# Scan inputs by VectorE for 20 of 32 units of a sequence, with scan tiles in place in a ring

## The chip, the cores and the metric

The program runs on one core of a Trainium2 chip (trn2). The metric is the device time of one execution in microseconds, as the median of several executions. One execution is also taken with a hardware profiler, which gives the page and the trace quoted here. The engines go by short names: PE is TensorE's matmuls and PEld its weight loads, DVE is VectorE, ACT is ScalarE, POOL is GpSimd and SP is SyncE, which here only issues DMAs.

## What is computed

The reference runs four blocks on four sequences of 256 tokens with width 512: latent attention, a gated feed-forward layer, a selective state-space layer, and a mixture of low-rank experts. The change is in the state-space layer, whose core is

```python
proj = hidden_states @ in_proj_w                 # x and z, 1024 channels each
xc = silu(causal_conv(x, taps=4) + conv_b)
ssm_p = einsum('bdl,ed->ble', xc, x_proj_w)      # 32 + 16 + 16 rows
dt_r, Bm, Cm = (rmsnorm(part) for part in split(ssm_p))
dt = softplus(einsum('blr,dr->bdl', dt_r, dt_proj_w) + dt_bias)
def step(h, inp):                                # h: 1024 channels x 16 states
    h = exp(dt_t[..., None] * A) * h + dt_t[..., None] * B_t[:, None, :] * x_t[..., None]
    return h, einsum('bdn,bn->bd', h, C_t)
y = (ys + D * xc) * silu(z)
```

Everything is in float32.

## The kernel before, in words

Attention and the feed-forward layer take the first third of the time; their last down-projection (L469) runs on into the first scans. After that the program is one loop over 128 *units* (`for u in range(total)`, L1342), 32 for each of the four sequences. A sequence has 8 chunks `c` of 128 channels; a chunk has 4 units `k` of 32 channels. A unit holds 32 channels x 4 state groups on the 128 partitions and 4 states x 256 time steps along the free dimension, so each of its tiles is 128 x 1024.

A unit goes through five steps:

- `decays(u)` on ScalarE (L967): four exponentials of dt times A, out of `dts`, which `spread` (L934) brings from DRAM as dt copied to the four state groups. They are emitted two units ahead.
- `scan_in(u)` on TensorE (L977): the input dt * x * B. `step_x` (L912, GpSimd) makes du = dt * x for a chunk, `step_turn` (L920) turns it with TensorE into `dut`, and 32 small matmuls of `dut` with `bdg`, a tile of B on diagonals that `b_diag` (L874) makes for each sequence, write the tile `bx` in PSUM. It has two buffers and is emitted one unit ahead.
- `scan(u)` on VectorE (L995): the recurrence over time, from `decay` (SBUF) and `bx` (PSUM) into `h` (SBUF).
- The product with C on GpSimd (L1000): `hc` = `h` * `crows`, where `c_rows` (L884, L887) spreads the rows of C over the partitions.
- `states_sum(q)` on TensorE (L1009), once for four units: sums over states into `ysum` (one PSUM tile), then `take_sum` on VectorE (L1014) adds D * xc. It is emitted in iteration 4q+5.

Around these, the loop has lists of other work for the next sequence and the previous one: `px_mm` (L759) and `pz_mm` (L942), the input projections; the convolution, `conv_in`, `conv_taps` and `conv_out`, whose mode is chosen by chunk (four matmuls with diagonals on TensorE at L815; three products on ScalarE at L803 and three sums on GpSimd at L818; or three multiply-adds on VectorE at L820); `pp_mm` (L845) with its norm; `step` (L900, L904), the step sizes with a softplus; `router`, `dense` and `expert_out` for the experts (L1030, L1096, L1101); `gate` (L1019); and the output projection `out_mm` (L1112). The order is written out by hand: `put(b, s, f, ...)` sets in which iteration, relative to sequence `b`, a piece is emitted. `first_at` pieces come first, then `decays(u+2)`, `scan_in(u+1)`, `soon_at` and `at` pieces, `scan(u)`, the sum, then `late_at` pieces. Each engine runs its pieces in that order. SP's queue is in order too: spreads of dt, weight loads of 512 KB (`w_in`), sends of dt to DRAM and results all stand in one row.

Of the kernel before, what the change touches and what calls it, by code (L numbers as in the profile page):

```python
# [28 lines left out]
NG = 4  # L29
# [12 lines left out]
def block_kernel(  # L42
# [587 lines left out]
    lnw = we.tile([64, 1], F32, name="lnw")  # L630
    dtw = we.tile([RK, DIN], F32, name="dtw")
# [15 lines left out]
    psx = ctx.enter_context(tc.tile_pool(name="psx", bufs=2, space=PSUM))  # L647
# [12 lines left out]
    def load_rest():  # L660
# [7 lines left out]
        nc.sync.dma_start(lnw, lnw_d)  # L668
        nc.sync.dma_start(dtw, dtw_d)
# [5 lines left out]
    csel = w1.tile([64, NU, P], F32, name="csel")  # L675
    nc.vector.tensor_copy(
        csel.rearrange("p g (n j) -> p (g n) j", n=NG),
        ident[0:64, RK + NST : RK + 2 * NST].unsqueeze(2).to_broadcast([64, NST, NB]),
    )
# [22 lines left out]
    ysum = psy.tile([P, S], F32, name="ysum")  # L702

    def odd(b):

        return act if b % 2 else w1

# [20 lines left out]
    def norm_scale(b):  # L728
# [4 lines left out]
        for i in range(2):  # L733
            t = act.tile([P, D], F32, tag="xnt", name="xnt", bufs=2)
# [28 lines left out]
    def mode(b, p, i):  # L763

        if b == 0:
            return "dve" if i == 0 else "act"
        return "pe" if i == 0 else "act" if p < 2 else "dve"
# [18 lines left out]
    def conv_in(b, p):  # L786
# [7 lines left out]
        for i in range(2):  # L794
# [5 lines left out]
            if m == "act":  # L800
                tp = live["tap"] = four()[:, 0 : (KC - 1) * S].rearrange("p (k t) -> p k t", k=KC - 1)
# [4 lines left out]
    def conv_taps(b, p):  # L806
        pad = pads[p % 2]
        for i in range(2):
            c, m = 2 * p + i, mode(b, p, i)
            xc = xcs[b][:, c, :]  # L810
            for k in range(KC if m == "pe" else KC - 1):
# [5 lines left out]
                elif m == "act":  # L817
                    nc.gpsimd.tensor_tensor(xc, xc, live["tap"][:, k, :], ALU.add)  # L818
# [22 lines left out]
    def pp_mm(b, h):  # L841
        if h == 0:
            live["pp"] = psmm.tile([P, 2, S], F32, tag="mm", name="pp")
        for c in range(h * HALF, (h + 1) * HALF):
            mm(live["pp"][:64, 0, :], lhsT=xpw[:, c, :], rhs=xcs[b][:, c, :],  # L845
               start=(c == 0), stop=(c == DC - 1))

    def pp_square(b):
        pp = live["pp"]
        sq = w1.tile([P, S], F32, tag="sq", name="sq")[:64]  # L850
        nc.scalar.activation(sq, pp[:64, 0, :], AF.Square)
        mm(pp[:64, 1, :], lhsT=cst[:64, C_BLK : C_BLK + 64], rhs=sq, start=True, stop=True)
        live["rs"] = w1.tile([P, S], F32, tag="sq", name="rs1")[:64]
        inv_root(live["rs"], pp[:64, 1, :], eps[:64, 1:2])

    def pp_norm(b):
        rs = live["rs"]
        nrms[b] = w1.tile([64, S], F32, tag="nrm", name="nrm")
        nc.vector.scalar_tensor_tensor(
            nrms[b], live["pp"][:64, 0, :], lnw[:, 0:1], rs, ALU.mult, ALU.mult  # L860
        )

    def b_turn(b):

        bt = live["bt"] = psmm.tile([P, 4, 8], F32, tag="mm", name="pbt")
        for t in range(4):
            for r in range(2):
                mm(bt[r * HT : (r + 1) * HT, t, :], lhsT=nrms[b][:, t * HT : (t + 1) * HT],
# [12 lines left out]
    def c_rows(b, i):  # L881
# [595 lines left out]
```

## Time and profile before

| What | Value |
|---|---|
| Median of 3 runs | 912.42 us (912.37 to 913.72) |
| Profiled execution, its own time | 917.66 us |
| Span in the profile | 915.9 us |
| Mean granted TensorE clock | 0.972 |
| Scans run from / to (starts) | 332.5 / 904.4 us |
| Scan (L995), one unit | 2.28 us, 128 units |
| Product with C (L1000), one unit | 2.37 us |
| Scan input (L977), all units | 149.1 us of TensorE |
| VectorE's wait for ysum ahead of L1014 | 146.8 us, 32 times |

The page gives busy time by engine, then slices of the span, then groups of instructions: line, engine, operation, tiles out<-in, shapes, count, then busy us and mean ns of one, then idle time just before them and what ended it. The stage view gives, for each stretch of the span, the busy time of each engine in it with the count of instructions, the granted clock, and the share and rate of DMA. The source view gives min/median/max ns of a line's instructions. The timeline gives start, duration, and how many neighbours are merged (x2).

### The profile page before, as it was taken

How to read it: one execution, taken by the hardware profiler on the slowest of the kernel's cores; microseconds unless marked ns; L12 is line 12 of the kernel's file. 1: busy time of each engine (PE TensorE's matmuls, PEld its weight loads, DVE VectorE, ACT ScalarE, POOL GpSimd, SP SyncE). 2: the span in 40 equal slices, each digit the busy share in tenths (PEclk: the TensorE clock that was granted, in tenths of full speed). 3: DMA queues.
4: the chain of work that ended last, by engine and by line, in shares of the span. 5: the costliest groups of instructions: out<-in, count | busy, mean ns of one | idle time of the engine just before them, and what ended most of it. 6: DMA issues, size and time to landing. Idle time of an engine off the chain costs nothing.

```text
span 915.9 us, 27817 instructions
## 1 busy us (share of the span) xinstructions
PE 860.5 (94%) x12468; PEld 556.3 (61%) x12468; DVE 530.8 (58%) x530; ACT 498.8 (54%) x985; POOL 443.9 (48%) x349
## 2 busy tenths in 40 slices
PE   5999999999999999999799999989999989898996
PEld 2665546665557677777555777545677645565553
DVE  4587554687344435657647647635565645656664
ACT  4335574345563753656773765764565665347541
POOL 3233320013332223685657676654576636657775
PEclk8899999999999989999999999989999989999899
DMA  6233420012333222344341350132323104021200
GB/s 207 80 108 94 119 73 12 1 35 70 81 85 107 38 74 79 96 131 126 103 136 43 95 152 26 48 105 61 102 81 97 29 23 128 26 82 49 59 4 25
DMA packets 48482, 70.74 MB, mean 77 GB/s; under 512 B 10173, under 2 KB 30409, under 8 KB 48234
## 3 DMA queue, kind: packets, MB, share of 16 engines
q1 hardware_dynamic: 38570, 48.77, 18.5%
q0 software_dynamic: 9072, 18.35, 7.1%
q8 instruction: 98, 1.61, 0.7%
q10 hardware_dynamic: 720, 1.84, 0.6%
q14 instruction: 22, 0.18, 0.1%
HBM read 52.42 MB, written 7.34 MB: 65 GB/s over the span
## 4 chain that ended last, share of the span: by engine, by line
PE 40%; ACT 4%; DVE 4%; POOL 3%; issue 1%; POOLq 0%; ACTq 0%; DVEq 0%
PE bx L977 9%; PE ysum L1009 6%; PE po L1112 5%; PE pz L942 5%; PE px L759 3%; PE po L1096 3%; DVE h L995 3%; PE ptu L920 3%; POOL hc L1000 2%; ACT decay L967 2%; PE pc L815 1%; PE pp L845 1%; DVE bdg L874 1%; PE pcr L884 1%; PE pdt L900 1%
## 5 line engine op out<-in xcount | busy, mean ns | idle before, releaser
L1000 POOL TENSOR_TENSOR hc<-h,cr 128x1024 f32<-128x1024 f32 (+1 forms) x130 | 302.3, 2333 | 221.3 <-PE ysum L1009 138.8
L995 DVE TENSOR_TENSOR_SCAN h<-decay,bx 128x1024 f32<-128x1024 f32 (+1 forms) x129 | 284.1, 2226 | 51.9 <-PE bx L977 36.6
L967 ACT ACTIVATE decay<-dts,aneg 128x255 f32<-128x255 f32 x504 | 212.3, 499 | 38.1 <-DVE h L995 29.7
L977 PE MATMUL bx<-bdg,dut 64*32 64x128 f32 x8192 | 149.1, 276 | 19.5 <-DVE h L995 10.3
L977 PEld LDWEIGHTS bx<-bdg,dut 64*32 64x32 f32 x8192 | 115.2, 106 | 73.9 <-issue 37.1
L1014 DVE SCALAR_TENSOR_TENSOR xc<-xc,vec,ysum 128x256 f32<-128x256 f32 (+1 forms) x33 | 15.6, 472 | 146.8 <-PE ysum L1009 146.8
L456 POOL TENSOR_TENSOR hlo<-g,hhi 128x512 fp32r<-128x512 f32 x28 | 35.9, 1283 | 114.2 <-ACT hhi L455 114.2
L354 DVE TENSOR_REDUCE mpl<-sc 128x4 f32<-128x1024 f32 x64 | 76.7, 1220 | 22.5 <-PE sc L352 21.0
L427 POOL DMA_DIRECT2D wgu<-in_wgu x56 | 31.2, 558 | 95.6 <-PE pg L444 94.4
L388 ACT ACTIVATE pe<-scT 128x1024 f32<-128x1024 f32 x64 | 64.0, 1023 | 22.9 <-PE sc L352 14.3
L1112 PE MATMUL po<-ow,xc 128*128 128x512 f32 x128 | 63.9, 619 | 2.8 <-POOL xc L1019 2.1
L1009 PE MATMUL ysum<-hc,stack 128*32 128x256 f32 x1024 | 66.5, 396 | 0.1
L923 ACT COPY dut<-ptu 128x512 f32<-128x512 f32 x32 | 18.7, 583 | 81.4 <-PE ptu L920 81.4
L942 PE MATMUL pz<-xn1T,w_in 128*128 128x256 f32 x256 | 62.7, 388 | 0.0
L759 PE MATMUL px<-xn1T,w_in 128*128 128x256 f32 x256 | 62.2, 388 | 0.0
L942 PEld LDWEIGHTS pz<-xn1T,w_in 128*128 128x128 f32 x256 | 46.9, 190 | 14.4 <-issue 9.4
L759 PEld LDWEIGHTS px<-xn1T,w_in 128*128 128x128 f32 x256 | 46.7, 189 | 9.8 <-issue 3.5
L1009 PEld LDWEIGHTS ysum<-hc,stack 128*32 128x32 f32 x1024 | 31.7, 113 | 32.6 <-issue 15.1
L444 PE MATMUL pg<-xhi,wgu 128*128 128x512 f32 x112 | 49.6, 443 | 1.4 <-ACT xhi L244 1.4
L469 PE MATMUL po<-wd,hhi 128*128 128x512 f32 x112 | 49.2, 439 | 0.0
L444 PE MATMUL pu<-xhi,wgu 128*128 128x512 f32 x112 | 47.3, 423 | 0.8 <-DVE g L454 0.8
L444 PE MATMUL pg<-xlo,wgu 128*128 128x512 f32 x112 | 45.1, 403 | 0.7 <-DVE xlo L251 0.7
(211 smaller groups left out, 1246.7 us busy)
## 6 DMA issues: line engine op xcount, KB each, us to landing
dts<-dtd SPq DMA_DIRECT2D x124, 128.0 KB, 2.9
wgu<-in_wgu POOLq DMA_DIRECT2D x56, 256.0 KB, 2.7
w_in<-in_inz SPq DMA_DIRECT2D x16, 512.0 KB, 4.8
w_in<-in_inx SPq DMA_DIRECT2D x14, 512.0 KB, 4.0
dtd<-dt SPq DMA_DIRECT2D x16, 256.0 KB, 3.1
wd<-in_wd POOLq DMA_DIRECT2D x7, 512.0 KB, 3.6
ow<-in_ow SPq DMA_DIRECT2D x8, 256.0 KB, 5.2
dg<-dgd SPq DMA_DIRECT2D x8, 256.0 KB, 4.5
```

The costliest lines, as they stand in the source:

```text
L354: nc.vector.tensor_reduce(mpl2[b % 2][:, qb, 2 * hp : 2 * hp + 2, 16 + 2 * gq : 18 + 2 * gq], sc.rearrange("p i (f k) -> p i f k", f=2), A ...
L388: nc.scalar.activation(pes[b, k][:, 2 * t : 2 * t + 2, :], sc, AF.Exp)
L444: mm(ps, lhsT=wgus[i][:, hc, :], rhs=xs[j][:, hc, :], start=(hc == 0 and j == 0), stop=(hc == HC - 1 and j == 1))
L469: mm(po, lhsT=hids[th][j][:, m, i * P : (i + 1) * P], rhs=wd[:, m, :], start=False, stop=(m == MC - 1 and j == 1))
L759: mm(px[:, i, :], lhsT=w[:, i, hc, :], rhs=xns[b][:, hc, :], start=(hc == 0), stop=(hc == HC - 1))
L942: mm(pz, lhsT=w[:, c % 2, hc, :], rhs=xns[b][:, hc, :], start=(hc == 0), stop=(hc == HC - 1))
L967: nc.scalar.activation(da[:, g, 1:], live["dts", b, c][:, k, 1:], AF.Exp, scale=aneg[:, c, k, g : g + 1])
L977: mm(bx[n * NB : (n + 1) * NB, 2 * r : 2 * r + 2, t * HT : (t + 1) * HT], lhsT=dut[b, c][w, t, k * NB : (k + 1) * NB], rhs=bdg[w, t, :, n, :],
L995: nc.vector.tensor_tensor_scan(h[:, n].rearrange("p n t -> p (n t)"), da[:, n].rearrange("p n t -> p (n t)"), bx[:, n].rearrange("p n t -> ...
L1000: (nc.vector if i == NG - 1 else nc.gpsimd).tensor_tensor(hc[:, n], h[:, n], crows[b][:, n, :], ALU.mult,)
L1009: mm(ysum[k * NB : (k + 1) * NB, :], lhsT=stack, rhs=hc[k][:, g, :], start=(g == 0), stop=(g == NU - 1))
L1112: mm(live["po", b, i], lhsT=xcs[b][:, c, i * P : (i + 1) * P], rhs=late_w["ow"][:, c, :], start=False, stop=(c == DC - 1))
```

## The change

- 12 of a sequence's 32 scan inputs stay on TensorE (`ON_PE`: units 0 and 2 of even chunks, unit 1 of odd chunks). For the other 20, VectorE multiplies rows of B (`brow`, new, in PSUM) with du spread over the partitions (`dus`, new, in SBUF) and writes the product into the scan tile in SBUF.
- `dus` comes by way of DRAM: `step_out` writes du (one DMA for each chunk), `step_spread` reads strips of 32 partitions (8 DMAs for even chunks, 12 for odd ones). Both are on SP's queue.
- `h`, `hc` and, for the 20, the scan input are one tile of a ring of seven (`ring`): the scan and the product with C write in place. `bx` in PSUM has one buffer in place of two; `brow` takes the bank space.
- `step_turn` turns only the columns of units that TensorE serves.
- `pp` and its norm are made twice, in partitions 0 to 63 and 64 to 127, so that the step sizes come from two row groups (partitions 0 to 31 and 64 to 95) and rows of B and C from two others (32 to 63 and 96 to 127), in `step` and `rows_bc`. `rows_bc` moves to iteration 31 from 26 and 27.
- The convolution of the next sequences has 3 chunks on TensorE (before: 4), 5 on ScalarE and GpSimd (2), none on VectorE (2).
- `scan_in(1)` is emitted after `scan(0)`; `step_x` moves two iterations ahead and its tile has one buffer.

The core of the diff:

```diff
-    psx = ctx.enter_context(tc.tile_pool(name="psx", bufs=2, space=PSUM))
+    psx = ctx.enter_context(tc.tile_pool(name="psx", bufs=1, space=PSUM))
     psy = ctx.enter_context(tc.tile_pool(name="psy", bufs=1, space=PSUM))
...
-    nc.vector.tensor_copy(
-        csel.rearrange("p g (n j) -> p (g n) j", n=NG),
-        ident[0:64, RK + NST : RK + 2 * NST].unsqueeze(2).to_broadcast([64, NST, NB]),
-    )
+    csel = w1.tile([P, NU, P], F32, name="csel")
+    for r, c in ((NB, RK), (3 * NB, 3 * NB + NST)):
+        nc.vector.tensor_copy(
+            csel[r : r + NB].rearrange("p g (n j) -> p (g n) j", n=NG),
+            ident[r : r + NB, c : c + NST].unsqueeze(2).to_broadcast([NB, NST, NB]),
...
     ysum = psy.tile([P, S], F32, name="ysum")
+    brow = psy.tile([P, NU, S], F32, name="brow")
 
     def odd(b):
 
         return act if b % 2 else w1
+
+    ON_PE = [((0, 2), (1,))[c % 2] for c in range(DC)]
 
     def exp_set():
...
             return "dve" if i == 0 else "act"
-        return "pe" if i == 0 else "act" if p < 2 else "dve"
+        return "pe" if i == 0 and p < NP - 1 else "act"
 
     dg_d = {}
...
         for c in range(h * HALF, (h + 1) * HALF):
-            mm(live["pp"][:64, 0, :], lhsT=xpw[:, c, :], rhs=xcs[b][:, c, :],
-               start=(c == 0), stop=(c == DC - 1))
+            for r in (0, HT):
+                mm(live["pp"][r : r + HT, 0, :], lhsT=xpw[:, c, :], rhs=xcs[b][:, c, :],
+                   start=(c == 0), stop=(c == DC - 1))
 
...
@@ -878,10 +885,12 @@
                 .to_broadcast([P, NST, HT]), ALU.mult,
             )
 
-    def c_rows(b, i):
+    def rows_bc(b, i):
         pc = psmm.tile([P, 2, S], F32, tag="mm", name="pcr")
         for j in range(2):
-            mm(pc[:, j, :], lhsT=csel[:, 2 * i + j, :], rhs=nrms[b], start=True, stop=True)
+            for r, out in ((NB, brow[:, 2 * i + j, :]), (3 * NB, pc[:, j, :])):
+                w = slice(r, r + NB)
+                mm(out, lhsT=csel[w, 2 * i + j, :], rhs=nrms[b][w], start=True, stop=True)
...
 
-    def step(b, p):
-        if p == 0:
+    def step(b, q):
+        if q == 0:
             dts[b] = w1.tile([P, DC, S], F32, tag="dt", name="dt")
-        pd = psmm.tile([P, 2, S], F32, tag="mm", name="pdt")
+        pds = [psmm.tile([P, 2, S], F32, tag="mm", name="pdt") for _ in range(2)]
         for i in range(2):
-            c = 2 * p + i
-            mm(pd[:, i, :], lhsT=dtw[:, c * P : (c + 1) * P], rhs=nrms[b][0:RK, :],
-               start=True, stop=True)
-        for i in range(2):
-            c = 2 * p + i
-            nc.scalar.activation(dts[b][:, c, :], pd[:, i, :], AF.Softplus, bias=vec[:, c, V_DB : V_DB + 1])
+            for k, pd in enumerate(pds):
+                c, w = 2 * q + 4 * k + i, slice(k * HT, k * HT + RK)
+                mm(pd[:, i, :], lhsT=dtw[w, c * P : (c + 1) * P], rhs=nrms[b][w], start=True, stop=True)
+        for k, pd in enumerate(pds):
+            for i in range(2):
+                c = 2 * q + 4 * k + i
+                nc.scalar.activation(dts[b][:, c, :], pd[:, i, :], AF.Softplus,
+                                     bias=vec[:, c, V_DB : V_DB + 1])
 
     def step_send(b, p):
         send("dt", b, p, dts[b][:, 2 * p : 2 * p + 2, :])
 
     def step_x(b, c, eng=nc.gpsimd):
 
-        live["du", c] = w1.tile([P, S], F32, tag="du", name="du", bufs=2)
+        live["du", c] = w1.tile([P, S], F32, tag="du", name="du")
         eng.tensor_tensor(live["du", c], dts[b][:, c, :], xcs[b][:, c, :], ALU.mult)
 
+    def step_out(b, c):
+        live["dud", b, c] = scr.tile([P, S], F32, tag="du", name="dud")
+        nc.sync.dma_start(live["dud", b, c], live["du", c])
+
     def step_turn(b, c):
 
-        du = live["du", c]
-        pt = psmm.tile([P, 4, P], F32, tag="mm", name="ptu")
+        du, ks = live["du", c], ON_PE[c]
+        n = len(ks)
+        cols = ident.rearrange("p (k j) -> p k j", k=NG)[:, ks[0] :: ks[1] - ks[0] if n > 1 else NG, :]
+        pt = psmm.tile([P, 4, n, NB], F32, tag="mm", name="ptu")
         for t in range(4):
             for r in range(2):
-                mm(pt[r * HT : (r + 1) * HT, t, :], lhsT=du[:, t * HT : (t + 1) * HT], rhs=ident,
+                mm(pt[r * HT : (r + 1) * HT, t], lhsT=du[:, t * HT : (t + 1) * HT], rhs=cols,
                    start=True, stop=True)
-        dut[b, c] = w1.tile([P, 4, P], F32, tag="dut", name="dut", bufs=2)
+        dut[b, c] = w1.tile([P, 4, n, NB], F32, tag="dut", name="dut", bufs=2)
         nc.scalar.copy(dut[b, c], pt)
+
+    def step_spread(b, c):
+        ks = [k for k in range(NG) if k not in ON_PE[c]]
+        t = live["dus", b, c] = w1.tile([P, len(ks), S], F32, tag="dus", name="dus", bufs=2)
+        for n in range(NG):
+            for i, k in enumerate(ks):
+                nc.sync.dma_start(t[n * NB : (n + 1) * NB, i, :],
+                                  live["dud", b, c][k * NB : (k + 1) * NB])
 
 
     def send(n, b, p, t):
...
     lent_d = ("d", "w_in", "d", "w_in")
-    NHC = 5
+    NHC = 7
 
     def lend(n, tag):
         pool, bufs = (we, 3) if tag == "w_in" else (w1, 2)
...
 
+    def ring(u):
+        if u < 4:
+            pool, tag, n = ((w1, "hc", 2), (w1, "hc", 2), (w1, "dg", 2), (we, "w_in", 3))[u]
+        else:
+            pool, tag, n = (act, "hc", NHC - 2) if (u - 4) % NHC < NHC - 2 else (w1, "hc", 2)
+        live["hc", u] = pool.tile([P, NG, S], F32, tag=tag, name="h", bufs=n)
+
     def scan_in(u):
         b, c, k = u // PER, u % PER // NU, u % NU
+        ring(u)
+        if k not in ON_PE[c]:
+            i = [j for j in range(NG) if j not in ON_PE[c]].index(k)
+            bx = live["bx", u] = live["hc", u]
+            nc.vector.tensor_tensor(
+                bx, brow, live["dus", b, c][:, i, :].unsqueeze(1).to_broadcast([P, NU, S]), ALU.mult
+            )
+            return
+        i = ON_PE[c].index(k)
         bx = live["bx", u] = psx.tile([P, NU, S], F32, tag="bx", name="bx")
         for t in range(4):
             for n in range(NG):
                 for r in range(2):
                     w = slice(r * HT, (r + 1) * HT)
                     mm(bx[n * NB : (n + 1) * NB, 2 * r : 2 * r + 2, t * HT : (t + 1) * HT],
-                       lhsT=dut[b, c][w, t, k * NB : (k + 1) * NB], rhs=bdg[w, t, :, n, :],
+                       lhsT=dut[b, c][w, t, i], rhs=bdg[w, t, :, n, :],
                        start=True, stop=True)
-
-    def hc_tile(u):
-        if u == 2:
-            return lend("hc", "dg")
-        if u % NHC < 2:
-            return lend("hc", "hc")
-        return act.tile([P, NG, S], F32, tag="hc", name="hc", bufs=NHC - 2)
 
     def scan(u, parts=1):
         b, c, k = u // PER, u % PER // NU, u % NU
-        da, bx = live.pop(("da", u)), live.pop(("bx", u))
-        h = lend("h", "w_in") if u < 3 else act.tile([P, NG, S], F32, tag="h", name="h", bufs=2)
-        hc = live["hc", u] = hc_tile(u)
+        da, bx, h = live.pop(("da", u)), live.pop(("bx", u)), live["hc", u]
         for i in range(parts):
             n = slice(i * NG // parts, (i + 1) * NG // parts)
             nc.vector.tensor_tensor_scan(
@@ -998,7 +1030,7 @@
             )
 
             (nc.vector if i == NG - 1 else nc.gpsimd).tensor_tensor(
-                hc[:, n], h[:, n], crows[b][:, n, :], ALU.mult,
+                h[:, n], h[:, n], crows[b][:, n, :], ALU.mult,
             )
 
     def states_sum(q, ks=range(NG), gs=range(NU)):
...
         for c in range(1, DC):
-            put_late(b, 4 * c - 4, step_x, b, c)
+            if c > 1:
+                put_late(b, 4 * c - 6, step_x, b, c)
+                put_late(b, 4 * c - 6, step_out, b, c)
+            if c > 1 or b:
+                put(b, max(4 * c - 4, 0), step_spread, b, c)
             put(b, 4 * c - 2, step_turn, b, c)
         for c in range(2, DC):
             put(b, 3 if c == 2 and not b else 4 * c - 6 + (not b), spread, "dt", b, c)
...
             put(b, 24, softplus_set)
-            for q in range(NP):
-                put(b, 24 + q // 2, step, nxt, q)
+            for q in range(2):
+                put(b, 24 + q, step, nxt, q)
             put(b, 25, exp_set)
-            for q in range(NP):
-                put(b, 26 + q, step_send, nxt, q)
-            put(b, 26, c_rows, nxt, 0)
-            put(b, 27, c_rows, nxt, 1)
-            put_late(b, 27, step_x, nxt, 0)
+            for i, q in enumerate((0, 2, 1, 3)):
+                put(b, 26 + i, step_send, nxt, q)
+            put(b, 31, rows_bc, nxt, 0)
+            put(b, 31, rows_bc, nxt, 1)
+            for c in range(2):
+                put_late(b, 26 + 3 * c, step_x, nxt, c)
+                put_late(b, 26 + 3 * c, step_out, nxt, c)
+            put(b, 28, step_spread, nxt, 0)
             put(b, 29, step_turn, nxt, 0)
             put(b, 28, spread, "dt", nxt, 0)
             put(b, 30, spread, "dt", nxt, 1)
...
             decays(u + 2)
-        if u + 1 < total:
+        if 0 < u < total - 1:
             scan_in(u + 1)
         for f, a in (*soon_at.get(u, ()), *at.get(u, ())):
             f(*a)
         scan(u, 1 if u < total - 1 else 4)
+        if u == 0:
+            scan_in(1)
         if u < 3:
             decays(u + 2)
         if u >= 5 and u % NU == 1:
```

## Prediction

> **What bounds the kernel now.** I read the page first: the engine shares, the forty slices, the costliest groups.
>
> ```profile
> PE 860.5 (94%) x12468; PEld 556.3 (61%) x12468; DVE 530.8 (58%) x530; ACT 498.8 (54%) x985; POOL 443.9 (48%) x349
> ...
> L1000 POOL TENSOR_TENSOR hc<-h,cr 128x1024 f32<-128x1024 f32 (+1 forms) x130 | 302.3, 2333 | 221.3 <-PE ysum L1009 138.8
> L995 DVE TENSOR_TENSOR_SCAN h<-decay,bx 128x1024 f32<-128x1024 f32 (+1 forms) x129 | 284.1, 2226 | 51.9 <-PE bx L977 36.6
> ...
> L977 PE MATMUL bx<-bdg,dut 64*32 64x128 f32 x8192 | 149.1, 276 | 19.5 <-DVE h L995 10.3
> ```
>
> TensorE is busy for 94% of the span; VectorE and GpSimd idle before their scan work, and what releases them is TensorE. A scan input (64 records, L977) costs TensorE 149.1/128 = 1.165 us.
>
> Then the table by stage, cut where scans start; units 4 to 126 of 128 run from 360.4 to 900.5.
>
> ```profile
> core 0: us, PE busy (x) PEld busy (x) DVE busy (x) ACT busy (x) POOL busy (x), PEclk, DMA share, GB/s
> 360.40:487.80 127.40, 119.13 (x2397) 83.67 (x2380) 81.33 (x70) 79.77 (x175) 83.66 (x52) 0.97 0.40 114
> 487.80:508.40 20.60, 19.73 (x401) 12.25 (x402) 13.48 (x13) 10.74 (x26) 13.75 (x8) 1.00 0.10 28
> 508.40:584.80 76.40, 74.65 (x1546) 53.44 (x1545) 47.44 (x30) 49.72 (x109) 50.10 (x30) 1.00 0.32 90
> 584.80:630.90 46.10, 42.90 (x709) 24.62 (x708) 21.39 (x15) 28.21 (x59) 26.49 (x18) 0.93 0.27 85
> ...
> 808.20:900.50 92.30, 86.91 (x1953) 52.62 (x1946) 56.50 (x32) 48.66 (x109) 64.06 (x36) 0.96 0.14 39
> ```
>
> In the middle of a sequence (18 units in 76.4 us) TensorE is 98% busy, so there it is the bound. At the seam (584.8 to 630.9, 8 units) every engine idles a little: a chain of softplus, table switches and decays on ScalarE, as the chain of waits shows.
>
> Last, the lines of VectorE that read two SBUF operands, beside GpSimd at the same moment (source view of L820 and L1014, then the timeline of VectorE and of GpSimd).
>
> ```profile
> L820 DVE SCALAR_TENSOR_TENSOR xc<-pad,vec,xc x27: 483/485/2480, 294.1 to 719.1; 128x256 f32<-128x256 f32 x27
> ...
> L1014 DVE SCALAR_TENSOR_TENSOR xc<-xc,vec,ysum x33: 340/480/482, 368.0 to 909.3; 128x256 f32<-128x256 f32 x31, 128x128 f32<-128x128 f32 x2
> ...
> 569.50 3.00 DVE L820 SCALAR_TENSOR_TENSOR xc<-pad,vec,xc 128x256 f32<-128x256 f32 x2 [0.19 <-ACT xc L798]
> ...
> 567.28 4.94 POOL L1000 TENSOR_TENSOR hc<-h,cr 128x1024 f32<-128x1024 f32 x2 [0.52 <-DVE h L995]
> ```
>
> The same operation and size never takes over 482 ns with one operand in PSUM (L1014), and up to 2480 ns with both in SBUF (L820). GpSimd ends at 572.22, VectorE at 572.50: the second L820 waited for a whole L1000. This, not any busy sum, is what I expect to decide.
>
> **What the Trainium skill says.** "SBUF — State Buffer", Who interferes with whom: a VectorE instruction with two SBUF inputs contends with a GpSimd instruction that reads SBUF; whichever starts first has the shared read port for the whole instruction. The lines above agree. "VectorE: DVE Perf Modes", The perf-mode tier table: a float32 tensor_tensor runs at one element a cycle, with or without PSUM; bdg (L874, 1024 elements, one operand in PSUM) takes 1.205 us. "TensorEngine Tiling (Array Packing)", Key Properties: different tiles run in parallel; L977 agrees, 64 records of 276 ns in 1.1 us. "DMA: Bandwidth & Descriptors", Anatomy of one DMA: a wait for a semaphore is made on the issuing sequencer, so it holds what is queued behind it; SP's L934 waits 201 us for decays here.
>
> **The change, part by part.** (1) TensorE loses 80 of 128 scan inputs: 80 x 1.165 = 93 us. Narrower ptu (32 x 1.09 us now; weight loads, 0.85 us each, stay): 0 to -22, I take -8. Steps in two row groups (20 us): 0 to -10, I take -5. One of four convolution chunks leaves (7.8 x 3 / 4): -6. Rows of B and the second half of pp: 0 if side by side, else +25; I take +5. Together about -107 us, spread over all stages.
>
> (2) VectorE gains 80 multiplications at 1.205 = 96 us and loses 18 L820 at 0.87 = 16 us; the middle stage goes from 47.4 to about 58 of 76.4 us.
>
> (3) GpSimd gains 9 chunks of taps x 3 x 0.73 = 20 us, less one dg of 1.1; ScalarE 9 x 3 x 0.50 = 14, less about 10 on narrower dut copies. Both have idle time for that.
>
> (4) The step no row of TensorE shows: 80 scans now have both inputs, decay and the ring tile, in SBUF; before, bx was in PSUM, and a scan took 2.28 us whatever GpSimd did. Each of the 80 now excludes the GpSimd products. What a hand-over costs comes from the pair above: a blocked L820 ended 0.28 us after GpSimd where it takes 0.485 alone, so 0.205 of its start is hidden, and a blocked scan needs 2.28 - 0.205 = 2.07 us after its turn comes. The second L1000 there ended 572.22, the first L820 569.985: 2.24 us a product. Tail operations (0.73 alone) about 0.60, by the same subtraction of 0.13. The multiplication itself has one SBUF operand and hides beside GpSimd.
>
> So the shared port is a sixth engine. Per unit: 2.24 + 20/32 x 2.07 = 3.53 us. Per stage: 3.53 x units, plus 0.82 x (GpSimd's busy time less 2.37 a unit, plus 6.6 of taps in stages of preparation):
>
> A 360.4 (28 units): 99.0 + 18.7 = 118 against 127.4 now
> B 487.8 (5): 19.2 against 20.6; 508.4 (18): 63.6 + 11.5 = 75.1 against 76.4; seam 584.8 (8): 34.4 against 46.1
> C 630.9 (6): 21.2 against 22.8; 653.7 (18, GpSimd 53.19): 77.6 against 82.4; seam 736.1 (8, GpSimd 23.02): 31.6 against 43.1
> D 779.2 (7): 25.1 against 29.0; 808.2 (24): 90.7 against 92.3
>
> Together 493 against 540. This floor needs a port that never idles. Two in-order queues take turns, each waits for the other's result, and VectorE stops every fourth unit for ysum (L1014, 147 us now), which now waits for a GpSimd that lags. TensorE as bound reaches 94 to 99% here; a coupled pair will do worse. I take 92% (between 98 and 85, an estimate): A's first 20 units 85.6/0.92 = 93, its last 8, a seam, 39; B 21 + 82 + 42; C 23 + 84 + 40; D 27 + 99. The seams lie between the port and today: TensorE gives 6 to 8 us back there, ScalarE's chain stays. Sum 550 against 540: +10. The start, up to 360, gains about 2 from shorter steps; the tail after 900.5 stays. Net +8.
>
> (5) New DMAs: 32 step_out and 320 step_spread on SP, at 0.43 to 0.61 us of issue (L934, L663), about 150 us of SP over 570; no compute waits for that in itself. What hangs on it: step_spread waits on SP for step_out's landing, behind it lie the spreads of dt and the weight loads. Cost taken as nothing; cover is the four to five units between step_x and the first multiplication (see rival three).
>
> (6) New waits, each taken at nothing. The multiplication on VectorE waits until the ring tile of seven units before is summed; L1014, ahead of it in the queue, has waited for that sum already. bx has one buffer: TensorE's next input waits for a scan two or three units back; behind it lie projections, which have slack now. du has one buffer: step_x of the next chunk, on GpSimd with the products behind it, waits for step_turn, emitted in the same iteration ahead of it; if TensorE is late there, products are late. The rows of C move from iterations 26 and 27 to 31: the first product of the next sequence waits for their copy on ScalarE, at most the 0.59 us of the copy and what lies ahead, four times.
>
> Profiled execution: 917.66 us with a span of 915.9, 5.2 above the median of 912.42. I apply the difference to the median: 912.4 + 8 = 920.
>
> **Rivals.** First, on the other side: the scan doesn't contend (its second operand, at two cycles an element, leaves gaps, or is read otherwise). Then each stage goes to the busiest engine at 93%: A 104, B 19 + 65 + 40, C 22 + 69 + 37, D 24 + 80 = 460, 82 less with the start: 828. For: no two-SBUF scan is in this trace. Against: L820 and L1014 differ in nothing but that. It decides if scans from SBUF stay at 2.28 us beside GpSimd. Second: the port is shared at 98%, because GpSimd always has a product waiting: A 126, B 20 + 77 + 41, C 22 + 79 + 39, D 26 + 93 = 523, with the start -19: 893. For: L820 shows strict alternation without gaps. Third: rows of du come late. step_x runs behind product 4c-6, its first reader in odd chunks is at unit 4c-1: five units, about 21 us. Writing takes 3.1, twelve issues 5.2 to 7.3, landing 2.9: 11 to 13 us. If GpSimd lags more than two units (8.6 us), VectorE waits; at 2 us for 16 odd chunks +32: 950.
>
> **Chances.** Port at about 92%: 0.47; no contention 0.13; port at 98%: 0.25; late rows 0.15. A measurement of this kernel tells about 0.2% from no change. Faster: 0.13 + 0.20 of the second + 0.06 of the first case = 0.39. Within 0.2%: 0.03 + 0.06 = 0.09. Slower: 0.52. The range runs from 886 to 952: it drops the no-contention case and a little of late rows; its ends are the port at 98% and at about 86%.
>
> **What would show it.** Right: scans with both operands in SBUF at 2.3 to 4.6 us with a mean near 3.5 or more, scans from PSUM still at 2.28; L1000's successor at more than 2.37 in the mean; TensorE under 85%. The middle stage near 4.5 us a unit. Wrong: scans from SBUF at 2.28 beside GpSimd, or VectorE waiting for DMA ahead of the multiplication, or a second TensorE bound.

## The result and the profile after

The changed kernel takes 956.35 us (median of 4 runs, 951.89 to 958.49) against 913.07 us for the kernel before on the same chip: a ratio of 1.046, 95% interval 1.041 to 1.051. It is slower, and by more than the forecast of 920 us; the top of the range, 952, is missed too. The profiled execution took 951.89 us with a span of 950.1, 34.2 us more than the span before. The stages take 575.8 us (540.1 before), the start 2.4 us less, and what follows the last cut 0.9 us more: 35.7 - 2.4 + 0.9 = 34.2. So all of the loss lies in the stages of the scan.

First the page of the kernel after: the engine shares, and the groups that answer to L1000, L995 and L977 of before.

```profile
PE 781.0 (82%) x7428; PEld 481.4 (51%) x7428; DVE 665.5 (70%) x593; ACT 501.9 (53%) x1012; POOL 568.5 (60%) x375
...
L1032 POOL TENSOR_TENSOR h<-h,cr 128x1024 f32<-128x1024 f32 (+1 forms) x130 | 354.3, 2740 | 118.7 <-DVE h L1027 105.4
L1027 DVE TENSOR_TENSOR_SCAN h<-decay,h 128x1024 f32<-128x1024 f32 (+1 forms) x81 | 235.5, 2936 | 0.0
L1027 DVE TENSOR_TENSOR_SCAN h<-decay,bx 128x1024 f32<-128x1024 f32 x48 | 109.1, 2274 | 5.4 <-PE bx L1018 3.5
L1008 DVE TENSOR_TENSOR h<-brow,dus 128x1024 f32<-128x1024 f32 x80 | 96.6, 1208 | 11.8 <-PE po L469 9.7
...
L1018 PE MATMUL bx<-bdg,dut 64*32 64x128 f32 x3072 | 61.1, 292 | 34.2 <-DVE h L1027 24.1
```

The same line of code, L1027, is two groups now. With the input in PSUM (`bx`) a scan takes 2.27 us as before; with the input in SBUF (`h`) the mean is 2.94 us. The product, 2.33 us before, has a mean of 2.74. TensorE is no longer the bound.

The source view of L1027 gives min/median/max ns and shows how cleanly the two kinds part:

```profile
L1027 DVE TENSOR_TENSOR_SCAN h<-decay,h x81: 665/2747/4395, 358.0 to 940.5; 128x1024 f32<-128x1024 f32 x77, 128x256 f32<-128x256 f32 x4
L1027 DVE TENSOR_TENSOR_SCAN h<-decay,bx x48: 2269/2272/2287, 330.5 to 927.6; 128x1024 f32<-128x1024 f32 x48
```

No scan from PSUM ever took over 2.287 us; one from SBUF took up to 4.395.

The stage table, cut at the same units as before (A 28 units, B 5 and 18, then D's last 24; with the seam between):

```profile
core 0: us, PE busy (x) PEld busy (x) DVE busy (x) ACT busy (x) POOL busy (x), PEclk, DMA share, GB/s
358.00:495.70 137.70, 101.82 (x1273) 67.66 (x1274) 107.89 (x81) 81.52 (x182) 113.08 (x61) 0.85 0.46 125
495.70:517.00 21.30, 19.56 (x236) 12.35 (x234) 19.00 (x15) 12.74 (x33) 14.64 (x7) 1.00 0.41 101
517.00:607.70 90.70, 63.72 (x781) 41.92 (x780) 65.13 (x35) 49.87 (x112) 72.82 (x39) 0.83 0.34 89
607.70:644.10 36.40, 31.02 (x394) 15.26 (x390) 30.91 (x19) 24.72 (x53) 36.15 (x18) 0.91 0.38 106
...
833.10:933.80 100.70, 72.94 (x970) 39.22 (x968) 82.15 (x46) 47.38 (x108) 87.42 (x36) 0.88 0.20 54
```

The middle stage of B (18 units) went from 76.4 to 90.7 us, the seam after it from 46.1 to 36.4. In the middle no engine is full: TensorE 70%, VectorE 72%, GpSimd 80%, and part of these last two is one engine waiting for the port with its instruction already counted as busy. So the engines wait for one another.

The waits of the whole span say for whom:

```profile
DVE xc L1046 <- PE ysum L1041: 117.7, 31, 12.7
...
POOL h L1032 <- DVE h L1027: 105.4, 38, 7.3
...
PE pp L851 <- ACT xc L841: 40.7, 3, 14.5
```

VectorE stands 117.7 us in all ahead of L1046 (adding D * xc to `ysum`), up to 12.7 us at a time, and what ends it is TensorE. One such stop, from the timelines of VectorE, GpSimd and TensorE in the middle of B:

```profile
530.42 4.05 DVE L1027 TENSOR_TENSOR_SCAN h<-decay,h 128x1024 f32<-128x1024 f32 x1
542.84 0.48 DVE L1046 SCALAR_TENSOR_TENSOR xc<-xc,vec,ysum 128x256 f32<-128x256 f32 x1 [8.37 <-PE ysum L1041]
...
536.58 2.34 POOL L823 TENSOR_TENSOR xc<-xc,dg 128x256 f32<-128x256 f32 x3
538.88 2.36 POOL L1032 TENSOR_TENSOR h<-h,cr 128x1024 f32<-128x1024 f32 x1
546.79 2.38 POOL L1032 TENSOR_TENSOR h<-h,cr 128x1024 f32<-128x1024 f32 x1 [5.56 <-DVE h L1027]
...
533.85 3.75 PE L820 MATMUL pc<-pad,dg 128*128 128x256 f32 x8 [6.40 <-DMA dg<-dgd]
537.53 1.43 PE L1018 MATMUL bx<-bdg,dut 64*32 64x128 f32 x64
538.89 1.99 PE L764 MATMUL px<-xn1T,w_in 128*128 128x256 f32 x8
540.81 1.93 PE L1041 MATMUL ysum<-h,stack 128*32 128x256 f32 x32
```

VectorE is done with its scan at 534.47. It waits until 542.84 because the sum (L1041) stands on TensorE behind a convolution that itself waited 6.4 us for a DMA, a scan input and a projection. GpSimd finishes its taps and the one product in stock at 541.24 and then has nothing until VectorE has made another scan. So the stop of one engine empties the other, and the read port that both need lies unused.

### The profile page after: what moved, and what is told of

The parts are those of the page before. It is cut to its first block, busy times and chain, and to the rows that moved or that the text cites. A ratio compares the mean times of both kernels' runs of the same rounds, so it can differ in the third digit from the quotient of the medians.

```text
span 950.1 us, 18408 instructions
## 1 busy us (share of the span) xinstructions
PE 781.0 (82%) x7428; PEld 481.4 (51%) x7428; DVE 665.5 (70%) x593; ACT 501.9 (53%) x1012; POOL 568.5 (60%) x375
## 5 line engine op out<-in xcount | busy, mean ns | idle before, releaser
L1032 POOL TENSOR_TENSOR h<-h,cr 128x1024 f32<-128x1024 f32 (+1 forms) x130 | 354.3, 2740 | 118.7 <-DVE h L1027 105.4
L1027 DVE TENSOR_TENSOR_SCAN h<-decay,h 128x1024 f32<-128x1024 f32 (+1 forms) x81 | 235.5, 2936 | 0.0
L1027 DVE TENSOR_TENSOR_SCAN h<-decay,bx 128x1024 f32<-128x1024 f32 x48 | 109.1, 2274 | 5.4 <-PE bx L1018 3.5
L1008 DVE TENSOR_TENSOR h<-brow,dus 128x1024 f32<-128x1024 f32 x80 | 96.6, 1208 | 11.8 <-PE po L469 9.7
L1041 PE MATMUL ysum<-h,stack 128*32 128x256 f32 x1024 | 81.5, 432 | 27.9 <-POOL h L1032 27.9
L1046 DVE SCALAR_TENSOR_TENSOR xc<-xc,vec,ysum 128x256 f32<-128x256 f32 (+1 forms) x33 | 15.5, 471 | 117.7 <-PE ysum L1041 117.7
L1018 PE MATMUL bx<-bdg,dut 64*32 64x128 f32 x3072 | 61.1, 292 | 34.2 <-DVE h L1027 24.1
L1018 PEld LDWEIGHTS bx<-bdg,dut 64*32 64x32 f32 x3072 | 46.6, 112 | 59.4 <-DVE h L1027 20.5
L1041 PEld LDWEIGHTS ysum<-h,stack 128*32 128x32 f32 x1024 | 35.4, 121 | 73.8 <-POOL h L1032 33.5
L1144 PE MATMUL po<-ow,xc 128*128 128x512 f32 x128 | 66.4, 643 | 2.5 <-POOL xc L1051 1.7
L923 POOL TENSOR_TENSOR du<-dt,xc 128x256 f32<-128x256 f32 x31 | 58.2, 1879 | 13.8 <-PE ptu L937 11.6
L823 POOL TENSOR_TENSOR xc<-xc,dg 128x256 f32<-128x256 f32 x54 | 49.1, 911 | 13.0 <-ACT dg L808 10.2
```

The lines of the kernel that those rows point to most:

```text
L923: eng.tensor_tensor(live["du", c], dts[b][:, c, :], xcs[b][:, c, :], ALU.mult)
L1008: nc.vector.tensor_tensor(bx, brow, live["dus", b, c][:, i, :].unsqueeze(1).to_broadcast([P, NU, S]), ALU.mult)
L1018: mm(bx[n * NB : (n + 1) * NB, 2 * r : 2 * r + 2, t * HT : (t + 1) * HT], lhsT=dut[b, c][w, t, i], rhs=bdg[w, t, :, n, :], start=True, sto ...
L1027: nc.vector.tensor_tensor_scan(h[:, n].rearrange("p n t -> p (n t)"), da[:, n].rearrange("p n t -> p (n t)"), bx[:, n].rearrange("p n t -> ...
L1032: (nc.vector if i == NG - 1 else nc.gpsimd).tensor_tensor(h[:, n], h[:, n], crows[b][:, n, :], ALU.mult,)
L1041: mm(ysum[k * NB : (k + 1) * NB, :], lhsT=stack, rhs=hc[k][:, g, :], start=(g == 0), stop=(g == NU - 1))
```

## The experiments

All times are medians beside the kernel before on the same chip, which lay between 914.9 and 916.8 us; ratios are to it, with the 95% interval. Runs came from several chips, so a difference of two medians is good to a few us. The theory at the start: the port is shared as forecast, and the rest of the loss comes from new waits in TensorE's and SP's queues. Its rival: the price of the port alone makes 956.

**The products into PSUM** (`e1_psum`). VectorE's product goes to the `bx` tile, so that no scan has both inputs in SBUF; the tile has one buffer, so each input is emitted after the scan ahead.

```diff
-            bx = live["bx", u] = live["hc", u]
+            bx = live["bx", u] = psx.tile([P, NU, S], F32, tag="bx", name="bx")
...
-        if 0 < u < total - 1:
-            scan_in(u + 1)
...
-        if u == 0:
-            scan_in(1)
+        if u < total - 1:
+            scan_in(u + 1)
```

> The 20 products of a sequence go to PSUM (the bx tile) in place of the ring tile, and every scan input is emitted after the scan ahead of it, since bx has one buffer; nothing else changes. No scan then has two SBUF inputs. Port theory: all scans at 2.28 us, GpSimd products at 2.37 us in the mean (2.79 in the changed kernel), du at 0.73 us (1.96); VectorE's own sum, 2.28 + 1.21 a unit and about 0.3 of other work, is the bound: 124 units x 3.8 = 470 us for the scans against about 580, so 850 to 890 us. Overload theory (VectorE simply has 96 us more to do): the multiplications are still there and now stand ahead of their own scan, so 945 to 965 us. Theory of late chains (taps and SP): GpSimd no longer lags, so they shrink too, 915 to 930 us, with scans and products still long if contention is not what made them long.

Measured: 933.58 us, 1.022 (1.019 to 1.026). All scans are back at one duration:

```profile
L1027 DVE TENSOR_TENSOR_SCAN h<-decay,bx x129: 659/2286/2289, 331.1 to 921.7; 128x1024 f32<-128x1024 f32 x125, 128x256 f32<-128x256 f32 x4
```

The contention is gone, but the time is in none of the three ranges expected, and the gain far less than the port theory asked for. The single tile now hands over between two engines: TensorE waits 96 us for scans before it can write `bx`, VectorE 44 us for TensorE's part. One wait took the other's place, so this run alone settles nothing.

**The convolution's modes as before** (`e2_taps`), which takes nine chunks of taps off GpSimd and ScalarE and puts three on TensorE, six on VectorE:

```diff
-        return "pe" if i == 0 and p < NP - 1 else "act"
+        return "pe" if i == 0 else "act" if p < 2 else "dve"
...
-                if q < NP - 2:
+                if q < NP - 1:
```

> The changed kernel with the convolution modes of the kernel before: four chunks of a sequence on TensorE, two on ScalarE and GpSimd, two on VectorE. Theory of late chains: the last chunk's six sums no longer stand on a lagging GpSimd ahead of silu, pp and ysum; the three stalls of 8 to 13 us of VectorE ahead of L1046 go, 20 to 35 us less, 922 to 936 us. Port theory alone: GpSimd loses 9 x 3 x 0.6 us of port time and VectorE's multiply-adds take 18 x 0.27 back, so about 10 us less, 945 us.

Measured: 949.62 us, 1.039 (1.036 to 1.041). The interval just touches that of the change, and the time is nearer to what the port theory expected (945).

**`step_out` later on SP** (`e4_out_late`). SP waited 230 us, 28 times, for du ahead of `step_out` (L927), with loads of `dg` and `w_in` behind it:

```diff
-                put_late(b, 4 * c - 6, step_out, b, c)
+                put(b, 4 * c - 4, step_out, b, c)
```

> The changed kernel with step_out of chunks 2 to 7 emitted in iteration 4c-4, just ahead of step_spread, in place of 4c-6; SP then waits there for a du that has long been made, so the dg and w_in loads are not held behind it. Theory of late chains: SP's 230 us of waiting for du shrink below 120, TensorE's waits for dg and w_in (17 us) go, 8 to 15 us less, 941 to 948 us. Port theory alone: within 4 us of 956. If strips of du then land late, VectorE waits for them ahead of the multiplication and the time rises by up to 20 us.

Measured: 949.93 us, 1.038 (1.035 to 1.041): between what the two theories expected, and the interval overlaps that of the change, so inconclusive by itself.

**Both of these edits** (`e24`).

> Both: convolution modes of before, and step_out late. If the forecast's price of the port was right and only the two chains were missed, 915 to 925 us (the forecast was 920). If the port costs more than forecast, 935 to 945 us.

Measured: 943.86 us, 1.033 (1.030 to 1.036). The two together take off 1.3 points, apart from the interval of the change. They are real and small: a third of the 36 us between the change and the forecast. The time is where it was expected if the port costs more than forecast. VectorE still waits 82 us for `ysum` in it.

**GpSimd writes without reading** (`e3_write`). Two memsets stand where the product with C was:

```diff
-            (nc.vector if i == NG - 1 else nc.gpsimd).tensor_tensor(
-                h[:, n], h[:, n], crows[b][:, n, :], ALU.mult,
-            )
+            if i == NG - 1:
+                nc.vector.tensor_tensor(h[:, n], h[:, n], crows[b][:, n, :], ALU.mult)
+            else:
+                for _ in range(2):
+                    nc.gpsimd.memset(h[:, n], 0.0)
```

> The changed kernel with GpSimd's product with C left out and two memsets of the same tile in its place (about 2.1 us against 2.37), so GpSimd is as busy and is waited for in the same way, but reads nothing from SBUF there; the states' product with C is missing from the result. Port theory (the shared thing is the read port): scans with both operands in SBUF fall to 2.28 us except beside taps, du and gates, and the time falls to 885 to 910 us. If GpSimd's occupation or the order of the work were the cause, the time stays above 940 us.

Measured: 888.74 us, 0.969 (0.964 to 0.974), as the port theory expected. The groups on the page of this run:

```profile
L1036 POOL MEMSET h<- 128x1024 f32 (+1 forms) x260 | 242.5, 937 | 164.3 <-DVE h L1027 149.8
...
L1027 DVE TENSOR_TENSOR_SCAN h<-decay,h 128x1024 f32<-128x1024 f32 (+1 forms) x81 | 185.3, 2317 | 0.0
...
L1048 DVE SCALAR_TENSOR_TENSOR xc<-xc,vec,ysum 128x256 f32<-128x256 f32 (+1 forms) x33 | 15.4, 466 | 107.6 <-PE ysum L1043 107.6
```

Scans from SBUF fall from a mean of 2.94 to 2.32 us beside an engine that still writes the same tiles. "SBUF — State Buffer", Who interferes with whom, in the Trainium skill says this: two SBUF inputs on VectorE contend with a GpSimd instruction that reads SBUF, not with one that only writes it. The pair of memsets is 0.5 us shorter than the product, so a part of the gain is plain work left out; and VectorE still waits 107.6 us for `ysum`, so that wait is there without the contention too.

**`take_sum` one unit later** (`e7_take_late`), to cover the stop with a scan; the gates move one iteration with it:

```diff
         if u >= 5 and u % NU == 1:
+            states_sum(u // NU - 1)
+        if u >= 6 and u % NU == 2:
             q = u // NU - 1
-            states_sum(q)
             take_sum(q // DC, q % DC)
```

> The changed kernel with take_sum (VectorE, L1046) one unit later, after scan 4q+6, and the gates that read it from 4c+6 on. Theory that the port stands idle because VectorE stops for ysum and GpSimd then has no product to make: VectorE's 118 us of waiting for ysum fall below 70, GpSimd's 105 us of waiting for scans fall too, 925 to 942 us. Theory that the port is simply full, or that a hand-over costs more than forecast: within 6 us of 956.

Measured: 960.03 us, 1.049 (1.044 to 1.054). The first theory is missed; the number of the second, within 6 us of 956, is met. The waits of this run, from 360 to 960 us:

```profile
POOL h L1032 <- DVE h L1027: 97.5, 41, 6.5
...
DVE h L1008 <- issue: 58.2, 12, 11.7
...
DVE h L1027 <- PE ysum L1041: 33.3, 8, 6.3
```

VectorE now stops further on: at scans, for the same late sum, and at the multiplication (L1008). The view names no releaser for that one; its ring tile is not free before the sum has read it, so the late sum is likely there too. GpSimd's wait is what it was (96.9 us in this window before the edit). So a later place on VectorE doesn't help; whether the sum itself is late is tested below. A ring of eight, which would loosen this, was not tried.

**All three edits** (`e247`: `e24` and the late `take_sum`).

> All three: convolution modes of before, step_out late, take_sum one unit later. If chains and stops are all that the forecast missed, and the hand-overs were priced right, 910 to 925 us (the forecast was 920). If something else is missing, above 930 us.

Measured: 953.70 us, 1.040 (1.036 to 1.045). No better than the second expectation, and 0.8 points worse than `e24`: VectorE waits ahead of L1008 (29.0 us for GpSimd, 24.4 without a releaser) and for the sum ahead of scans (29.6 us).

**All 32 products by VectorE, into PSUM** (`e5_all_dve`): the products of `e1_psum` without TensorE's share, so that VectorE alone fills and empties the tile; no turned du and no diagonals of B, `dus` by four DMAs a chunk, with the late `take_sum`.

```diff
-    ON_PE = [((0, 2), (1,))[c % 2] for c in range(DC)]
+    ON_PE = [() for c in range(DC)]
...
-            bx = live["bx", u] = live["hc", u]
+            bx = live["bx", u] = psx.tile([P, NU, S], F32, tag="bx", name="bx")
...
-        return "pe" if i == 0 and p < NP - 1 else "act"
+        return "pe" if i == 0 else "act"
...
-            put(b, 4 * c - 2, step_turn, b, c)
```

> A version that takes TensorE out of scan inputs altogether: all 32 products of a sequence by VectorE into PSUM (as in e1_psum), so step_turn, its copies and the diagonals of B go, du comes by 4 DMAs a chunk, one convolution chunk more on TensorE than in the changed kernel, take_sum one unit later. Port theory: no scan contends and no scan waits for TensorE's single buffer; VectorE is the bound with 2.29 + 1.23 + 0.17 a unit and about 0.3 of other work: 3.9 to 4.0 a unit against 4.4 before, 855 to 885 us. Overload theory: VectorE has 58 us more than in the changed kernel, so 960 us or more.

Measured: 854.85 us, 0.933 (0.930 to 0.937), at the lower end of what the port theory expected (855 to 885), and faster than both kernels.

**The same with the product in SBUF** (`e10_dve_sbuf`). Against `e5_all_dve` one line differs:

```diff
-            bx = live["bx", u] = psx.tile([P, NU, S], F32, tag="bx", name="bx")
+            bx = live["bx", u] = live["hc", u]
```

> e5_all_dve with one thing changed: VectorE writes its 32 products of a sequence into the ring tile in SBUF (as the changed kernel does for 20) in place of PSUM. Instructions, order, DMAs and TensorE's work are those of e5_all_dve (855 us). Port theory: each of 128 scans now excludes GpSimd: 2.15 us a scan and 2.15 a product, which is what blocked ones take in the changed kernel's trace, plus gates, du and taps, about 4.3 x 122 + 60 = 585 us at best between units 4 and 126 against 486, so 955 to 1010 us. Any theory in which the port doesn't matter (VectorE's load, order, DMAs): within 10 us of 855.

Measured: 995.39 us, 1.087 (1.084 to 1.090), inside the port theory's range. The scans and the multiplications on the page of `e5_all_dve`, which write and read PSUM:

```profile
L1025 DVE TENSOR_TENSOR_SCAN h<-decay,bx 128x1024 f32<-128x1024 f32 (+1 forms) x129 | 288.0, 2234 | 13.6 <-PE po L469 1.4
...
L1006 DVE TENSOR_TENSOR bx<-brow,dus 128x1024 f32<-128x1024 f32 x128 | 157.8, 1233 | 7.5 <-PE pcr L892 3.1
```

and on the page of `e10_dve_sbuf`:

```profile
L1025 DVE TENSOR_TENSOR_SCAN h<-decay,h 128x1024 f32<-128x1024 f32 (+1 forms) x129 | 419.6, 3255 | 12.7 <-ACT decay L990 4.3
...
L1006 DVE TENSOR_TENSOR h<-brow,dus 128x1024 f32<-128x1024 f32 x128 | 153.2, 1197 | 40.0 <-PE ysum L1039 37.3
```

Where one operand lies costs 140.5 us, on the same work by the same engines; 131.6 us of it is the longer scans (419.6 against 288.0). Between units 4 and 126 a scan from SBUF or a GpSimd instruction is running for 606 of 626 us in this trace (while one waits for the other, the other runs, so this is the time for which the port is held). This shows the shared port as the bound; the product itself costs hardly more into PSUM (1.233 against 1.197 us).

**`e5_all_dve` with `take_sum` back in its place** (`e11_dve_take`), the last hunk of `e7_take_late` undone.

> e5_all_dve with take_sum and the gates back where the changed kernel has them. Tells what the later take_sum is worth where the ring does not bind first: if VectorE's stop for ysum costs time wherever it is, 31 stops of 1 to 2 us, 880 to 900 us; if it is hidden, within 6 us of 855.

Measured: 864.12 us, 0.945 (0.941 to 0.948): 9 us more than `e5_all_dve`, between the two theories. With no scan input in the ring, the late `take_sum` does help. The wait for the sum in this run:

```profile
DVE xc L1044 <- PE ysum L1039: 25.6, 10, 4.6
```

**The sum ahead of the listed pieces** (`e12_sum_first`). Against the changed kernel only the place of `states_sum` on TensorE differs: in iteration 4q+5 it is emitted before the projections, convolutions and other pieces of that iteration, in place of after them.

```diff
+        if u >= 5 and u % NU == 1:
+            states_sum(u // NU - 1)
         for f, a in (*soon_at.get(u, ()), *at.get(u, ())):
...
             q = u // NU - 1
-            states_sum(q)
             take_sum(q // DC, q % DC)
```

> The changed kernel with states_sum emitted ahead of the listed pieces of iteration 4q+5 in place of behind them, so TensorE makes ysum as soon as GpSimd's last product of the group is there; take_sum stays where it is. Theory that the port stands idle because VectorE stops for ysum (and GpSimd then runs out of products): the 118 us of waiting ahead of L1046 fall to 60 to 90, and 10 to 25 us go, 931 to 946 us. Theory that the port is full whatever VectorE waits for: within 4 us of 956. If TensorE then waits for GpSimd with its projections behind it, up to 10 us slower.

Measured: 918.82 us, 1.004 (1.002 to 1.005), better than either theory expected: 37.5 us less than the change. Its waits, from 360 to 960 us:

```profile
POOL h L1032 <- DVE h L1027: 59.6, 29, 4.3
DVE xc L1046 <- PE ysum L1041: 55.8, 23, 5.5
PE ysum L1041 <- POOL h L1032: 51.4, 21, 5.5
```

Both waits fall together, VectorE's by 61.9 us and GpSimd's by 37.3. Now the sum waits for GpSimd's product, as it must, and no more for TensorE's other work. The scans from SBUF still run to 4.39 us: the port is as contended as before, but it is used. Counted from the two traces, between units 4 and 126, a scan from SBUF or a GpSimd instruction is running for 516 us, against 518 in the change; neither is running for 25 us, against 58. So the move took away idle time of the port; the time for which it is held stayed as it was.

**With the edits of `e24` too** (`e13_three`).

> The same with the convolution modes of before and step_out late (e24, 944 us). If these stops are what is left between 944 and the forecast of 920, 920 to 934 us; if the port is simply used to 85% in this order of work, 940 to 948 us.

Measured: 914.63 us, 1.000 (0.998 to 1.001), below both expectations. Only 0.4 points less than `e12_sum_first`, where the same two edits took 1.3 off the change: most of their gain seems to have come by way of the late sum.

**The same move in the kernel before** (`b1_sum_first`).

> The kernel before, with the one move of e12_sum_first: states_sum ahead of the listed pieces of iteration 4q+5. VectorE waits 147 us for ysum there too. If that wait costs only where VectorE and GpSimd share the bound, nothing changes while TensorE is the bound: 909 to 918 us. If it costs wherever it is, 20 to 40 us go, as in the changed kernel. TensorE may then wait for GpSimd's product, up to 10 us slower.

Measured: 910.42 us, 0.994 (0.992 to 0.995). VectorE's wait for the sum halves; the line of the wait view in the kernel before, then in this run:

```profile
DVE xc L1014 <- PE ysum L1009: 146.8, 32, 7.2
...
DVE xc L1014 <- PE ysum L1009: 70.6, 27, 4.3
```

and the kernel gains 6.4 us of these 76, inside the first expectation. Where TensorE is the bound, VectorE's wait was nearly free.

**The same move in `e11_dve_take`** (`e14_dve_sum_first`).

> e11_dve_take (all products by VectorE into PSUM, 864 us) with states_sum ahead of the listed pieces; take_sum where the changed kernel has it. VectorE is the bound there, so stops for ysum should count: as good as or better than the later take_sum of e5_all_dve, 846 to 856 us. If the stops cost nothing there, 860 to 868 us.

Measured: 839.71 us, 0.918 (0.915 to 0.920), the best of all and better than expected. The wait for the sum fell from 25.6 us to

```profile
DVE xc L1044 <- PE ysum L1039: 2.6, 3, 2.2
```

and the time by 24.4 us: here the wait counted in full.

## Why the prediction was wrong, step by step

**(1) TensorE loses about 107 us.** It lost 79.5 (860.5 to 781.0). The scan inputs gave 88.0 (149.1 to 61.1), the narrower `ptu` 13.3, the steps 7.5. The convolution chunk gave 2.0 for 6. The second half of `pp` and the rows of B cost 11.4 where 5 was taken, and records that wait for a product or run at a lower clock are longer (L1041 66.5 to 81.5). No harm came of it: TensorE isn't the bound.

**(2) and (3), the busy sums.** The multiplications cost 96.6 us against 96 forecast, at 1.208 us each, and never waited for the port. The taps cost GpSimd 29 us more, not 20 (L823 0.91 us each against 0.74 for L818 before). The du products (L923) grew by 35 us (58.2 against 22.9), which no term has: the shortest took 0.72 us, the median 2.71, since most stand behind a scan. That is waiting counted as busy time. Whether "idle time for that" was a fair reading, `e2_taps` and `e24` say: the taps alone are worth some 0.7 points, at the edge of what the intervals separate.

**(4) The shared port, the mechanism.** Right in kind, and right in size for a turn. Of 79 whole scans from SBUF, 60 were blocked; each ended 2.147 us after the GpSimd instruction ahead of it (forecast 2.07). A product that waited for such a scan ended 2.151 us after it (forecast 2.24). The sum of a turn is 4.30 us; 4.31 was forecast. `e10_dve_sbuf` against `e5_all_dve`, and `e3_write`, show the cause. Two of the signs named came out otherwise: the mean of a scan from SBUF is 2.94 us, not 3.5 or more, and the middle stage took 90.7 / 18 = 5.04 us a unit, not 4.5.

**(4) The floor of the port: the step that failed.** The term that was mis-sized is the stages' sum, 576 us for 550: 26 of the 34 us by which the profiled execution grew; the other 8 were forecast. The prediction made it of a floor, 493, and of time in which the port is idle, 57 ("I take 92%"). In the trace, counted between units 4 and 126, a scan from SBUF or a GpSimd instruction is running for 518 us, and neither for 58. So the floor was 25 us too low, and the idle time came out as forecast. The prediction priced every instruction as if it stood behind the other engine, with its start hidden. Only 27 of 122 products stood behind a scan for long, and most of the others took their full 2.37 us; a scan that did stand behind GpSimd held the port for 2.15 us, not 2.07. In the mean a scan held it for 2.16 us (2.07 forecast, +7 us in all), a product for 2.29 (2.24, +8), and the smaller GpSimd instructions came to 72 us (62, +10).

By stage, measured and (forecast): A 100.3 (93) and 37.4 (39); B 21.3 (21), 90.7 (82), 36.4 (42); C 25.3 (23), 92.1 (84), 40.0 (40); D 31.6 (27), 100.7 (99). The seams came out at or under the forecast. In the middle of B the port was held for 79.4 us (75.1 forecast) and idle for 11.3.

**(4) The idle time: right in size, by luck.** Its 57 us were a rough factor, and the cause that the prediction gives was wrong. "VectorE stops every fourth unit for ysum (L1014, 147 us now), which now waits for a GpSimd that lags." In the trace TensorE's sum waited only 27.9 us for GpSimd, VectorE 117.7 us for TensorE. The sum was held by TensorE's own queue, where it stands behind the pieces of its iteration. The 147 us were on the page before and cost little there, since VectorE had time; the prediction counted the stop as part of the factor in place of following the queue. `e12_sum_first` changes that place alone: the idle time falls from 58 to 25 us, the time by 37.5 us to 918.8. So most of the idle time that the forecast took as given could be avoided. That this run is so near the forecast of 920 is luck: a floor 23 us higher than forecast (516) and an idle time 32 us shorter.

**(5) New DMAs, "cost taken as nothing".** Perhaps not nothing. SP stood 230 us ahead of `step_out`, and loads of `dg` and `w_in` behind it came late to TensorE (12.4 and 4.3 us of its waits). What it costs by itself isn't settled: `e4_out_late` gives 0.8 points, with intervals that overlap. With the sum ahead, it and the taps together are worth 0.4 points.

**(6) New waits, "each taken at nothing".** The multiplication's wait for its ring tile cost nothing in the change, as argued, because L1046 ahead of it had waited already. It is there all the same: `e7_take_late` took that cover away and met it. The wait for the single `bx` cost TensorE 24.1 us, off the bound. VectorE waited 3.5 us for `bx`.

**The rivals.** No contention (828) fell with the source view. Late rows of du (950) gave nearly the measured time, but by another way: in the trace VectorE waited 1.2 us in all for `dus`. The time of a rival being right is no evidence for it. The port at 98% (893) needed a GpSimd that always has a product in stock; it ran out 38 times, for 105.4 us. Two sums of the prediction are a little off, without weight for the result: it has 893 for the port at 98%, but 886 as the end of the range for it, and 920 + 32 is 952, not 950.

**What stays open.** What leaves the port idle for the last 25 us in `e12_sum_first`, between the products for which the sum waits (51.4 us) and the scans for which GpSimd waits (59.6), wasn't taken apart. Nor was an order of work looked for in which more instructions stand behind one another and the floor comes nearer to 493. To put the sum still earlier, in iteration 4q+4, wasn't tried either.

## What to carry to other kernels

A wait that is free while another engine is the bound becomes a cost once the change makes the waiting engine the bound: of the wait that the same move took away, 6.4 us of 76 counted before, 37.5 of 62 in the change, 24.4 of 23 in `e14_dve_sum_first`. So when work moves from one engine to another, go through the waits of the one that gets it, find in the releasing engine's queue what stands ahead of the release, and price it in full. When two engines share something, price an instruction with its start hidden only where it will really stand behind the other; here the forecast was 25 us short by that. And consider putting an operand of VectorE in PSUM where GpSimd reads SBUF beside it: with VectorE alone filling the tile that choice was worth 140 us, with TensorE filling it too (`e1_psum`) 23.

## What the runs showed of the hardware that was not expected

TensorE's granted clock fell as TensorE had less to do. It was 0.972 before, with TensorE busy for 94% of the span, 0.919 after with 82%, and 0.853 in `e10_dve_sbuf` with 75%; in the middle of B it went from 1.00 to 0.83. "TensorE: Matmul & The Clock Gate", Part 1, in the Trainium skill tells of a block that sets the clock by how busy TensorE has been of late, and the three runs go that way; the forecast didn't allow for it. Records of unchanged work were longer: L1144, the output projection, took 643 ns a record where L1112 took 619, and L1018 292 where L977 took 276. What this did to the total wasn't measured.

The hand-over of the read port is even: a waiting scan and a waiting product both end 2.15 us after the other engine's instruction, though alone they take 2.28 and 2.37. So 0.13 and 0.22 us of each, by this subtraction, lie hidden in the wait.
